# Linear attention with a gated FFN: attention's last product from eight quarter products to seven

## The chip, the cores and the metric

The kernel runs on one core of a Trainium2 chip. The metric is the device time of one execution in microseconds (us), as the median of several runs; a profiled execution of the same kernel gives the trace. Five engines work side by side, each through its own queue in order: TensorE (PE: matmuls and transposes; PEld is its weight load), VectorE (DVE), ScalarE (ACT), GpSimd (POOL) and SyncE (SP), from whose queue most transfers are issued.

## The reference, cut to what matters

The input `src` has 4 batch entries of 2048 tokens with 256 features, in float32. What is computed (16 heads of 64, `HD` = 1024; weights given, all biases and gains at work):

```
xn  = layernorm(src)
Q   = elu(xn Wq + bq) + 1 ;  K = elu(xn Wk + bk) + 1 ;  v = xn Wv + bv
KV  = per head and batch entry: sum over tokens of K^T v
Z   = 1 / (Q . sum over tokens of K + 1e-6)          per token and head
att = (Z Q KV) Wo + bo
x1  = layernorm(xn + att) * g1 + be1
s   = layernorm(x1 + gelu(x1 W1 + b1) W2 + b2) * g2 + be2
g   = silu( fp4_linear( silu(fp4_linear(xn, w_gate)) * fp4_linear(xn, w_up), w_down ) )
out = src + s * g
```

`fp4_linear` rounds its input and its weight to a grid of eight magnitudes, with one scale for each 16 values. KV needs all tokens of an entry before the first `att` of that entry can be computed.

## The kernel before, in words

**Tiling.** The tokens are worked on in 32 blocks `n` of 256 (two halves of 128, `TB` = 2), 8 for each of the entries `b = n // 8`. KV and Wo are multiplied together once per entry: M = blockdiag(KV) Wo is a 1024 x 256 matrix, and `att` of a block is (Z Q) M. M is kept in two tiles `m` of 128 x 4 x 256, one for each half `f` of the heads (`m_of_half`, L589-643; half 0 from four of the eight 128-row chunks of M, half 1 from the others).

**Stages.** A prologue computes the keys of entry 0 and quantizes the weights. Then the main loop (L1093-1222) runs over the 32 blocks. Beside block n of entry b < 3 it works on the keys of entry b+1, so that KV of the next entry is ready when its first block comes: two steps (`subs`) a block, first for the first half of the heads over the first four blocks, then for the second half over the last four, so n % 8 = 0 to 3 have other work beside them than n % 8 = 4 to 7. The last entry (n = 24 to 31) has no keys beside it.

TensorE executes everything in the order in which the program gives it (`mm`, L102, and `tr`, L105, keep the program order), so a block on TensorE is this sequence, with the names by which the profile knows the products:

- `pq` (L793): the block's queries from `xnT` and `wq_sb`, ahead of which stands `ffn_1` of the block before (`pf`, L877, first product of the FFN: `x1T` x `w1_sb`; ScalarE applies gelu to it and writes `hT`);
- `pk` (`keys_k`, L567) for the first step of keys, `pz` (`sums`, L815): the sums that Z is made of. VectorE adds epsilon and inverts, the result goes to DRAM (`z_d`) and comes back spread over partitions as `zb`;
- `pxk` (keys times values' inputs), `pg` (`gate_up` of block n+1, L732), `pd` (`down`, L757);
- then `qz` (L842) on VectorE: `zq <- zq * zb`, two operations of 128 x 1024. `zq` is Z Q, transposed;
- `pk` for the second step of keys, and on VectorE `kk` from it;
- `pa` (`attention`, L849): (Z Q) M, 16 products of 128 x 128 by 128 x 256 into one accumulator;
- `pxk` again, `py` (`ffn_2`, L924, second product of the FFN of block n-1), `pt_x` (`x1_T`, L865: x1 transposed), `pscale` (`spread_scales`: the scales of the fp4 grid, transposed, to DRAM and back), the rest of `py`, and `ffn_1`.

**VectorE and ScalarE** keep the program order in the prologue. In the main loop (`in_order` is False) a scheduler places their operations, and `issue_after` holds one behind a named other. Behind `pa` VectorE adds `xn` to it (`x1`), takes the statistics (`stats`; the power for 1/sqrt runs on GpSimd, `rstd` L430) and normalizes. `scales_h` and `scales_x` (L661) compute the scales of the fp4 grid for the next blocks: `scales_x(n + 2)` reads the tile `xn` of block n+2, which `load_xn` (L648) fetches on SP into the buffer that the sum for `x1` has just freed (two buffers). `keys_in` and `keys_apart` prepare the next step of keys: statistics and normalization on VectorE, or a fetch of what the first half already stored, then on ScalarE a column of ones and two copies (`apart`), and on SP a transposing transfer (`apartT`).

**The FFN's second product** is computed by seven products of quarters instead of eight: `w2_sums` (L218) forms four sums of quarters of W2 once on GpSimd, `ffn_sums` (L905) four sums of quarters of `hT` per block on VectorE (tile `hs`), `ffn_2` 28 products of 128 columns into seven quarters of two accumulators (`PY_SLOT`, L922), and `output` (L948) adds them with five additions (`s<-s,py`). The attention product is not computed in that way here.

**GpSimd** does the power for rstd, `gate_addend` (L778), `ffn_addend` (L785) and `attention_addend` (L652): additions and multiplications of 128 x 512. **Accumulators** (PSUM): a pool `mm` of four, a pool `acc` of two, a pool `pxk` of two.

Of the kernel before, what the change touches and what calls it, by code (L numbers as in the profile page):

```python
# [8 lines left out]
F32 = mybir.dt.float32  # L9
# [3 lines left out]
ALU = mybir.AluOpType  # L13
AX = mybir.AxisListType

P = 128
# [6 lines left out]
def linear_attention_gated_by_fp4_ffn(  # L23
# [38 lines left out]
    nc = tc.nc  # L62
    B, S, D = src.shape
# [5 lines left out]
    NH = HD // P  # L69
# [4 lines left out]
    TB = 2  # L74
# [14 lines left out]
    def mm_tile(name):  # L89
        return ps.tile([P, 512], F32, tag="mm", name=name)  # L90

    def acc_tile(name, tag="acc"):
        return pacc.tile([P, 512], F32, tag=tag, name=name)
# [8 lines left out]
    def mm(*args, **kw):  # L102
        return tc.keep_in_program_order(nc.tensor.matmul(*args, **kw))  # L103
# [105 lines left out]
    def w2(q):  # L209
        return w2_sb[:, W2_OF[q]]  # L210
# [375 lines left out]

    kh, m_sb = {}, {}

    def m_of_half(b, f, dep=None, ahead=False):  # L589


        nm = f"{b}_{f}"
        if wv_sb.get(f) is not None:
            wv = wv_sb.pop(f)
        else:
            wv = batch.tile([P, ND, HALF], F32, tag="wv", name=f"wv_{nm}", bufs=1)
            nc.sync.dma_start(wv, wv_d[f])
        wo = batch.tile([P, 4, D], F32, tag="wo", name=f"wo_{nm}", bufs=1)
        load_when(dep, wo, by_chunks(Wo)[:, 4 * f : 4 * f + 4, :])
        if ahead:  # L600
            yield
        if f == 0:
            kh[b] = batch.tile([P, NH, 32], F32, tag="kh", name=f"kh_{b}")
            nc.gpsimd.memset(kh[b], 0.0)
        m = m_sb[b, f] = batch.tile([P, 4, D], F32, tag="m", name=f"m_{nm}", bufs=3)
        pxk = keys.pop((b, "pxk", f))
        xk = batch.tile([P, ND, HALF], F32, tag="xk", name=f"xk_{nm}", bufs=1)
        for d in range(ND):
            scalar.copy(xk[:, d, :], pxk[d])

        k_d = dram.tile([1, HALF], F32, tag="k_d", name=f"k_d_{nm}", bufs=2)
        nc.sync.dma_start(k_d, xk[:1, 0, :])
        yield
        cols_ = k_d.rearrange("o (c i p) -> i p (o c)", c=4, i=2)
        for i in range(2):
            hs = slice(i * DH, (i + 1) * DH)
            nc.sync.dma_start(kh[b][hs, 4 * f : 4 * f + 4, 2 * f + i], cols_[i])
        yield

        pkv = mm_tile(f"pkv_{nm}")[:, : 4 * DH].rearrange("p (c f) -> p c f", c=4)  # L620
        kv = work.tile([P, 4, P], F32, tag="s", name=f"kv_{nm}", bufs=1)
        nc.gpsimd.memset(kv, 0.0)
        for ci in range(4):
            for d in range(ND):
                for h in range(2):
                    cs = slice(ci * P + h * DH, ci * P + (h + 1) * DH)
                    mm(
                        pkv[h * DH : (h + 1) * DH, ci, :], wv[:, d, cs], xk[:, d, cs],
                        start=d == 0, stop=d == ND - 1,
                    )  # L630
        for h in range(2):
            hs = slice(h * DH, (h + 1) * DH)
            scalar.copy(kv[hs, :, hs], pkv[hs])
        yield
        for c2 in range(2):
            pm = mm_tile(f"pm_{nm}_{c2}").rearrange("p (c d) -> p c d", c=2)
            for ci in range(2):
                mm(
                    pm[:, ci, :], kv[:, 2 * c2 + ci, :], wo[:, 2 * c2 + ci, :],
                    start=True, stop=True,  # L640
                )
            scalar.copy(m[:, 2 * c2 : 2 * c2 + 2, :], pm)
        yield


# [196 lines left out]
    def qz(n):  # L842
# [3 lines left out]
            ins = vector.tensor_tensor(zq[:, cs, :], zq[:, cs, :], zb[:, cs, :], ALU.mult)  # L846
        return ins.ins

    def attention(n):  # L849
        zq = blk[n].pop("zq")  # L850
        m = [m_sb[n // NB, f] for f in range(2)]
        pa = acc_tile(f"pa_{n}").rearrange("p (j d) -> p j d", j=TB)
        for j in range(TB):
            for c in range(NH):
                mm(
                    pa[:, j, :], zq[:, c, j * P : (j + 1) * P], m[c // 4][:, c % 4, :],
                    start=c == 0, stop=c == NH - 1,
                )
        x1 = work.tile([P, TB, D], F32, tag="x1", name=f"x1_{n}")
        vector.tensor_tensor(x1, blk[n].pop("xn"), pa, ALU.add)  # L860
        mv, rstd = stats(x1, f"1_{n}")
        normalize(x1, x1, mv, rstd)
        blk[n]["x1"] = x1
# [31 lines left out]
                )  # L895
        blk[n]["gelu"] = ins.ins

    def ffn_sums(n):  # L905
        hT = blk[n]["hT"]
        h = {
            f"{i + 1}{k + 1}": hT[:, k * NF2 : (k + 1) * NF2, i * P : (i + 1) * P]
            for i in range(2) for k in range(2)
        }  # L910
        t = work.tile([P, 4, NF2, P], F32, tag="zb", name=f"hs_{n}", bufs=1)
        s1, s2, s3, s4 = (t[:, i] for i in range(4))
        vector.tensor_tensor(s3, h["11"], h["21"], ALU.subtract)
        vector.tensor_tensor(s1, h["21"], h["22"], ALU.add)
        vector.tensor_tensor(s2, s1, h["11"], ALU.subtract)
        vector.tensor_tensor(s4, h["12"], s2, ALU.subtract)
        blk[n]["ffn"] = {
            1: (h["11"], "11"), 2: (h["12"], "21"), 3: (s4, "22"), 4: (h["22"], "t4"),
            5: (s1, "t1"), 6: (s2, "t2"), 7: (s3, "t3"),
        }  # L920

    PY_SLOT = {2: (0, 0), 3: (0, 1), 4: (0, 2), 1: (0, 3), 6: (1, 0), 7: (1, 1), 5: (1, 2)}  # L922

    def ffn_2(n, to, order=(1, 2, 4, 3, 5, 7, 6)):  # L924

        py = blk[n].setdefault("py", {})
        done = blk[n].get("done", 0)
        blk[n]["done"] = to
        for at in range(done, to):
            i, c = order[at // NF2], at % NF2  # L930
            bank, slot = PY_SLOT[i]
            if bank not in py:

                t = (mm_tile if (bank == 0) == (n >= NBLK - NB - 1) else acc_tile)(f"py{bank}_{n}")
                py[bank] = t.rearrange("p (s d) -> p s d", s=4)
            if "ffn" in blk[n]:
                h, w = blk[n]["ffn"][i]
            else:
                hT = blk[n]["hT"]
                h, w = {  # L940
                    1: (hT[:, :NF2, :P], "11"), 2: (hT[:, NF2:, :P], "21"),
                    4: (hT[:, NF2:, P:], "t4"),
                }[i]
            mm(
                py[bank][:, slot, :], h[:, c, :], w2(w)[:, c, :], start=c == 0, stop=c == NF2 - 1
            )

    def output(n):  # L948
        g, o, x1, py = (blk[n][k] for k in ("g", "o", "x1", "py"))
        s = work.tile([P, TB, D], F32, tag="s", name=f"s_{n}", bufs=1)  # L950

        def quarters(t):
            return t.rearrange("p j (h d) -> p (j h) d", h=2)

        def of(bank, slot, n):
            return py[bank][:, slot : slot + 1, :].to_broadcast([P, n, P])

        s4, x4 = quarters(s), quarters(x1)
        vector.tensor_tensor(s4, x4, py[0], ALU.add)
        vector.tensor_tensor(s4[:, :3, :], s4[:, :3, :], of(0, 3, 3), ALU.add)  # L960
        vector.tensor_tensor(s4[:, 1:, :], s4[:, 1:, :], of(1, 0, 3), ALU.add)
        vector.tensor_tensor(s4[:, 2:, :], s4[:, 2:, :], of(1, 1, 2), ALU.add)
        vector.tensor_tensor(s4[:, 1::2, :], s4[:, 1::2, :], of(1, 2, 2), ALU.add)
        mv, rstd = stats(s, f"2_{n}")
        for j in range(TB):
            vector.scalar_tensor_tensor(
                s[:, j, :], s[:, j, :], mv[:, j, 0:1], g[:, j, :], ALU.subtract, ALU.mult
            )
        for j in range(TB):
            vector.scalar_tensor_tensor(  # L970
                o[:, j, :], s[:, j, :], rstd[:, j : j + 1], o[:, j, :], ALU.mult, ALU.add
            )
        nc.sync.dma_start(rows_of(out, n), o)
# [119 lines left out]
    for n in range(NBLK):  # L1093
# [56 lines left out]
                down(n, j)  # L1150
        with tc.issue_after(blk[n + 1]["late"]) if n < last else nullcontext():
            qz_ins = qz(n)
        if not subs:
            ffn_2(n - 1, 4 if n < last else 8)
        kk_ins = keys_k(b + 1, subs[1]) if subs else qz_ins
        if n > 0:
            with tc.issue_after(kk_ins):
                ffn_sums(n - 1)
        attention(n)
        if n + 2 < NBLK:  # L1160
            load_xn(n + 2)
        if subs:
# [16 lines left out]
                scales_x(n + 2)  # L1179
        for sub in next_subs if n == 0 else ():  # L1180
            keys_in(bn + 1, sub)
        early = [sub for sub in next_subs[:1] if sub < NB]
        for sub in early:
            keys_apart(bn + 1, sub)
        x1_T(n)
        if not subs:
            ffn_addend(n, False)
        if n == last:
            gate_addend(n)
        for sub in next_subs[len(early) :]:  # L1190
            keys_apart(bn + 1, sub, blk[n]["act"])

        if n > 0 and not subs:
# [63 lines left out]
```

## Time and profile before

| what | value |
|---|---|
| median of 3 runs | 1907.02 us (1906.78 to 1907.91) |
| the profiled execution: its own time | 1906.97 us |
| its span in the trace | 1904.9 us |
| its granted TensorE clock | 0.997 of full speed |
| all chunks of `pa`, 1024 records | 227.0 us busy |
| VectorE busy / ScalarE busy / GpSimd busy | 1303.2 / 708.9 / 357.5 us |

The span is the time from the first to the last instruction on the core; the execution's own time has about 2 us around it. "Busy" adds up an engine's working time, and says nothing of whether its idle time cost anything. A float32 product appears in the trace as two records: 16 products of `pa` per block give 32 records, and 32 blocks 1024. In the groups of instructions, `pa<-m,zq 128*128 128x256 f32` reads: output `pa` from the inputs `m` and `zq`, a 128 x 128 weight against a moving operand of 128 partitions by 256 columns; behind it stand busy time and mean ns of one (the ends of pipelined matmuls are modelled, so for products the distance between starts is the better measure), and then the engine's idle time ahead of the group with what ended most of it. In a timeline line stand the start in us, the duration, the engine, the line and operation, how many of them are drawn together, and in brackets how long the engine had stood idle and for what.

### The profile page before, as it was taken

The page shows a single profiled execution, that of the slowest core. Times are in us where ns is not written, and L with a number is a line of the kernel's source. Part 1 is how long each engine was busy: PE and PEld are TensorE (multiplying, and loading weights), DVE is VectorE, ACT ScalarE, POOL GpSimd, SP SyncE. Part 2 cuts the span into 40 slices and gives each one's busy share as a digit, 9 for nine tenths or more (in the row PEclk, how much of TensorE's full clock was granted, in tenths as well). Part 3 has the DMA queues.
Part 4 walks back from the last instruction along what each step waited for, and adds up shares of the span by engine and source line. Part 5 has one row for each costly group of instructions (what it writes and reads, how often), then busy time and mean ns, then how long its engine had stood idle before and what let it go on. Part 6 is the DMA issues. An engine that isn't in the chain of part 4 may idle for free.

```text
span 1904.9 us, 23848 instructions
## 1 busy us (share of the span) xinstructions
PE 1875.4 (98%) x8772; PEld 1379.3 (72%) x8772; DVE 1303.2 (68%) x2338; ACT 708.9 (37%) x1191; POOL 357.5 (19%) x348
## 2 busy tenths in 40 slices
PE   9999999999999999999999999999999999999997
PEld 4456577767777777777777787677777688788876
DVE  5657667666666667666666666676666678888875
ACT  2334444334334344433243543353332333333332
POOL 1411222011121112220112210212110122222221
PEclk9999999999999999999999999999999999999999
DMA  5525555345434456544444553464442444445541
GB/s 182 190 78 112 116 105 108 97 106 96 93 64 89 110 102 126 132 80 95 88 87 78 115 103 102 91 137 89 95 83 69 78 80 88 82 84 93 91 81 42
DMA packets 228243, 187.62 MB, mean 98 GB/s; under 512 B 107656, under 2 KB 189844, under 8 KB 228127
## 3 DMA queue, kind: packets, MB, share of 16 engines
q1 hardware_dynamic: 227292, 184.53, 46.4%
q8 instruction: 69, 1.13, 0.3%
q10 hardware_dynamic: 834, 1.58, 0.3%
q14 instruction: 48, 0.39, 0.1%
HBM read 130.91 MB, written 32.59 MB: 86 GB/s over the span
## 4 chain that ended last, share of the span: by engine, by line
PE 90%; DVE 4%; DMA 2%; issue 1%; POOL 1%; ACT 0%; SPq 0%; POOLq 0%; ACTq 0%; DVEq 0%
PE pg L103 15%; PE pk L103 11%; PE pa L103 11%; PE pxk L103 11%; PE pf L103 11%; PE pq L103 11%; PE pd L103 8%; PE py L103 8%; PE pz L103 2%; DMA zb<-z_d 1%; DVE x L119 1%; DVE scale L119 1%; PE pt_x L106 1%; POOL rstd L430 1%; PE pm L103 1%
## 5 line engine op out<-in xcount | busy, mean ns | idle before, releaser
L430 POOL TENSOR_TENSOR rstd<-rstd,neg_half 128x2 f32<-128x2 f32 x96 | 72.6, 757 | 1450.2 <-DVE rstd L119 1015.0
L103 PE MATMUL pg<-wgu,qT 128*128 128x352 f32 x1024 | 311.0, 462 | 2.3 <-issue 2.2
L103 PEld LDWEIGHTS pg<-wgu,qT 128*128 128x128 f32 x1024 | 194.6, 191 | 120.2 <-issue 17.9
L103 PE MATMUL pk<-wk_sb,xnT_k 128*128 128x512 f32 x512 | 232.2, 596 | 1.5 <-ACT xnT_k L119 1.4
L103 PE MATMUL pf<-x1T,w_sb 128*128 128x256 f32 x1024 | 226.9, 380 | 3.6 <-DVE zq L119 2.7
L103 PE MATMUL pa<-m,zq 128*128 128x256 f32 x1024 | 227.0, 379 | 1.9 <-DVE zq L119 1.8
L103 PE MATMUL pq<-xnT,wq_sb 128*128 128x256 f32 x1024 | 226.5, 379 | 1.0 <-ACT hT L119 1.0
L103 PE MATMUL pxk<-kk,xn_k 128*128 128x512 f32 x496 | 227.4, 597 | 0.0
L103 PEld LDWEIGHTS pa<-m,zq 128*128 128x128 f32 x1024 | 193.5, 190 | 39.4 <-issue 11.2
L103 PEld LDWEIGHTS pq<-xnT,wq_sb 128*128 128x128 f32 x1024 | 194.3, 190 | 27.7 <-ACT hT L119 1.4
L103 PEld LDWEIGHTS pf<-x1T,w_sb 128*128 128x128 f32 x1024 | 191.8, 190 | 29.7 <-DVE zq L119 3.1
L119 DVE SCALAR_TENSOR_TENSOR kk<-ek,pk 128x512 f32<-128x512 f32 x128 | 85.9, 686 | 146.8 <-ACT ek L119 146.8
L103 PEld LDWEIGHTS pk<-wk_sb,xnT_k 128*128 128x128 f32 x512 | 97.5, 191 | 104.6 <-issue 97.8
L103 PE MATMUL pd<-wd,qT 128*128 128x256 f32 x768 | 172.8, 380 | 0.5 <-ACT wd L119 0.5
L119 ACT ACT_TABLE_LOAD x122 | 156.5, 1283 | 41.3 <-PE pk L103 26.3
L103 PEld LDWEIGHTS pd<-wd,qT 128*128 128x128 f32 x768 | 145.3, 190 | 25.7 <-DVE qT L119 1.6
L103 PEld LDWEIGHTS pxk<-kk,xn_k 128*128 128x128 f32 x496 | 91.3, 190 | 99.0 <-issue 92.1
L119 ACT ACTIVATE h<-pg 128x352 f32<-128x352 f32 x128 | 58.8, 460 | 213.3 <-PE pg L103 213.3
L119 DVE TENSOR_TENSOR h<-h,pg 128x352 f32<-128x352 f32 x128 | 66.1, 517 | 100.7 <-PE pg L103 99.2
L119 ACT ACTIVATE hT<-pf,bcol 128x256 f32<-128x256 f32 x256 | 105.7, 472 | 57.8 <-PE pf L103 57.1
L119 ACT ACTIVATE ek<-pk,neg_one 128x512 f32<-128x512 f32 x128 | 85.5, 686 | 110.0 <-PE pk L103 109.7
L103 PE MATMUL py<-w_sb,hs 128*128 128x128 f32 x1024 | 125.9, 275 | 0.0
(136 smaller groups left out, 2327.5 us busy)
## 6 DMA issues: line engine op xcount, KB each, us to landing
zb<-z_d SPq DMA_DIRECT2D x128, 256.0 KB, 6.0
qT<-scale_d SPq DMA_DIRECT2D x248, 128.0 KB, 5.4
x_k<-in_L_attn_src_dram SPq DMA_DIRECT2D x32, 256.0 KB
x<-in_L_attn_src_dram SPq DMA_DIRECT2D x32, 256.0 KB, 2.6
xn_d<-xn_k SPq DMA_DIRECT2D x32, 256.0 KB, 2.0
xn<-xn_d SPq DMA_DIRECT2D x32, 256.0 KB, 2.6
xnT_d<-xnT_k SPq DMA_DIRECT2D x32, 256.0 KB, 2.0
xnT<-xnT_d SPq DMA_DIRECT2D x32, 256.0 KB, 2.8
```

The lines of the kernel that those rows point to most:

```text
L103: return tc.keep_in_program_order(nc.tensor.matmul(*args, **kw))
L106: return tc.keep_in_program_order(nc.tensor.transpose(*args, **kw))
L119: ins = op(*args, **kw)
L430: pool["last"] = nc.gpsimd.tensor_tensor(rstd[:, j0:j1], rstd[:, j0:j1], neg_half[:, j0:j1], ALU.pow).ins
```

## The change

In entries 0, 1 and 2 (`in_seven`) attention's product takes the form that the FFN's second product already has; the last entry keeps the eight.

- `m_sums(b)`: when the second half of M is ready, GpSimd forms t1 to t4 from M's quarters, four operations of 128 x 512, once per entry. `m` becomes two tags: `m0` with two buffers for the first half of the heads, `m1` with one for the second, and a tile `mt` for three of the sums; t1 is written over a quarter of M.
- `attention_sums(n)`: right behind `qz`, VectorE forms four sums of quarters of `zq` (128 x 512 each), three into a new tile `zs` and one over a quarter of `zq`.
- `attention(n)`: 28 products of 128 columns in place of 16 of 256, into two accumulators (one from `acc`, one from `mm`), and five additions in place of one for `x1`.
- Order: in block 0 attention goes ahead of the second step of keys. `keys_apart` of the next block's first step was called ahead of `x1_T`; now all of them follow it, behind `x1T` on ScalarE.
- The FFN's product is written with the same helpers as before in other words (`halves`, `seven_sums`, `seven_products`, `add_seven`); of its sums the order of the first two changes.

```diff
+    def in_seven(b):
+        return b < B - 1
+
+    def m_sums(b):
+        m = {
+            f"{k + 1}{j + 1}": m_sb[b, k][:, :, j * P : (j + 1) * P]
+            for k in range(2) for j in range(2)
+        }
+        t = batch.tile([P, 3, 4, P], F32, tag="mt", name=f"mt_{b}", bufs=1)
+        t1, (t2, t3, t4) = m["12"], (t[:, i] for i in range(3))
+        nc.gpsimd.tensor_tensor(t3, m["22"], m["12"], ALU.subtract)
+        nc.gpsimd.tensor_tensor(t1, m["12"], m["11"], ALU.subtract)
+        nc.gpsimd.tensor_tensor(t2, m["22"], t1, ALU.subtract)
+        nc.gpsimd.tensor_tensor(t4, m["21"], t2, ALU.subtract)
+        m_sb[b] = {"11": m["11"], "21": m["21"], "22": m["22"], "t1": t1, "t2": t2, "t3": t3, "t4": t4}
...
-        m = m_sb[b, f] = batch.tile([P, 4, D], F32, tag="m", name=f"m_{nm}", bufs=3)
+        m = m_sb[b, f] = batch.tile([P, 4, D], F32, tag=f"m{f}", name=f"m_{nm}", bufs=2 - f)
...
+        if f > 0 and in_seven(b):
+            m_sums(b)
         yield
...
+    SLOT = {2: (0, 0), 3: (0, 1), 4: (0, 2), 1: (0, 3), 6: (1, 0), 7: (1, 1), 5: (1, 2)}
+    WEIGHT = {1: "11", 2: "21", 3: "22", 4: "t4", 5: "t1", 6: "t2", 7: "t3"}
+    FOUR = NH // 2
...
+    def seven_sums(h, s1, s2, s3, s4):
+        vector.tensor_tensor(s1, h["21"], h["22"], ALU.add)
+        vector.tensor_tensor(s3, h["11"], h["21"], ALU.subtract)
+        vector.tensor_tensor(s2, s1, h["11"], ALU.subtract)
+        ins = vector.tensor_tensor(s4, h["12"], s2, ALU.subtract)
+        return {1: h["11"], 2: h["12"], 3: s4, 4: h["22"], 5: s1, 6: s2, 7: s3}, ins.ins
+
+    def seven_products(banks, left, weights, order, lo, hi):
+        for at in range(lo, hi):
+            i, c = order[at // FOUR], at % FOUR
+            bank, slot = SLOT[i]
+            mm(
+                banks[bank][:, slot * P : (slot + 1) * P], left[i][:, c, :],
+                weights(WEIGHT[i])[:, c, :], start=c == 0, stop=c == FOUR - 1,
+            )
+
+    def add_seven(dst, x, banks):
...
+        s4, x4 = quarters(dst), quarters(x)
+        vector.tensor_tensor(s4, x4, banks[0].rearrange("p (s d) -> p s d", s=4), ALU.add)
+        vector.tensor_tensor(s4[:, :3, :], s4[:, :3, :], of(0, 3, 3), ALU.add)
+        vector.tensor_tensor(s4[:, 1:, :], s4[:, 1:, :], of(1, 0, 3), ALU.add)
+        vector.tensor_tensor(s4[:, 2:, :], s4[:, 2:, :], of(1, 1, 2), ALU.add)
+        vector.tensor_tensor(s4[:, 1::2, :], s4[:, 1::2, :], of(1, 2, 2), ALU.add)
+
+    def attention_sums(n):
+        h = halves(blk[n].pop("zq"))
+        t = work.tile([P, 3, FOUR, P], F32, tag="zs", name=f"zs_{n}", bufs=1)
+        blk[n]["zs"], ins = seven_sums(h, t[:, 0], t[:, 1], h["21"], t[:, 2])
+        return ins
...
     def attention(n):
...
         x1 = work.tile([P, TB, D], F32, tag="x1", name=f"x1_{n}")
-        vector.tensor_tensor(x1, blk[n].pop("xn"), pa, ALU.add)
+        xn = blk[n].pop("xn")
+        b = n // NB
+        if in_seven(b):
+            pa = [acc_tile(f"pa0_{n}"), mm_tile(f"pa1_{n}")]
+            seven_products(
+                pa, blk[n].pop("zs"), lambda q: m_sb[b][q], (1, 2, 4, 3, 5, 7, 6), 0, 7 * FOUR
+            )
+            add_seven(x1, xn, pa)
...
             qz_ins = qz(n)
+        if in_seven(b):
+            attention_sums(n)
         if not subs:
             ffn_2(n - 1, 4 if n < last else 8)
+        if n == 0:
+            attention(n)
         kk_ins = keys_k(b + 1, subs[1]) if subs else qz_ins
         if n > 0:
             with tc.issue_after(kk_ins):
                 ffn_sums(n - 1)
-        attention(n)
+            attention(n)
...
-        early = [sub for sub in next_subs[:1] if sub < NB]
-        for sub in early:
-            keys_apart(bn + 1, sub)
         x1_T(n)
...
-        for sub in next_subs[len(early) :]:
+        for sub in next_subs:
             keys_apart(bn + 1, sub, blk[n]["act"])
```

## Prediction before the run

> **What bounds the kernel now.** I read the page's busy shares first, then busy time by stage (one block per stretch), then the groups by form, and last the timeline of single blocks, because only there one sees which wait ends last.
>
> ```profile
> PE 1875.4 (98%) x8772; PEld 1379.3 (72%) x8772; DVE 1303.2 (68%) x2338; ACT 708.9 (37%) x1191; POOL 357.5 (19%) x348
> ```
> ```profile
> core 0: us, PE busy (x) PEld busy (x) DVE busy (x) ACT busy (x) POOL busy (x), PEclk, DMA share, GB/s
> 474.44:531.54 57.10, 57.10 (x263) 42.10 (x262) 37.36 (x64) 19.59 (x34) 9.27 (x8) 1.00 0.45 89
> 649.71:706.81 57.10, 57.10 (x263) 42.10 (x262) 40.05 (x78) 24.08 (x40) 10.65 (x10) 1.00 0.53 105
> ```
> TensorE is busy for all of a middle block (57.10 of 57.10 us, clock 1.00): each us taken from its queue is a us gained, and each wait put into it is a us lost. VectorE has 17 to 20 us free per block, but that is a sum; what counts is where it stands when TensorE needs it.
>
> ```profile
> L103 PE MATMUL pa<-m,zq 128*128 128x256 f32 x1024 | 227.0, 379 | 1.9 <-DVE zq L119 1.8
> L119 DVE SCALAR_TENSOR_TENSOR o<-s,rstd,o 128x256 f32<-128x256 f32 x64 | 88.5, 1420 | 18.8 <-POOL rstd L430 18.8
> L119 DVE TENSOR_TENSOR s<-s,py 128x384 f32<-128x384 f32 x64 | 35.3, 551 | 29.2 <-PE py L103 28.2
> ```
> The first row is the product to be replaced, 32 records a block. The second (1420 ns, where the like-sized s<-s,mv,g takes 486) shows VectorE while GpSimd works on 128x512 operands: about 0.93 us more for each operation. The third is what an addition from PSUM costs.
>
> Block 4 of the timeline (entry 0, the first block beside which the second half of the next keys is worked on):
>
> ```profile
> 409.33 1.22 DVE L119 TENSOR_TENSOR zq<-zq,zb 128x1024 f32<-128x1024 f32 x1 [3.47 <-DMA zb<-z_d]
> 415.68 0.89 DVE L119 SCALAR_TENSOR_TENSOR h<-h,rs_h 128x704 f32<-128x704 f32 x1
> 417.18 7.07 PE L103 MATMUL pa<-m,zq 128*128 128x256 f32 x32
> 417.73 1.28 DVE L119 SCALAR_TENSOR_TENSOR kk<-ek,pk 128x512 f32<-128x512 f32 x2 [1.15 <-ACT ek L119]
> 424.09 3.60 PE L103 MATMUL pxk<-kk,xn_k 128*128 128x512 f32 x8
> 424.29 0.69 DVE L119 TENSOR_TENSOR x<-xn,pa 128x512 f32<-128x512 f32 x1 [2.62 <-PE pa L103]
> 425.00 0.32 SPq L650 DMA_DIRECT2D xn<-xn_d  x1
> 427.00 0.74 DVE L119 TENSOR_SCALAR x<-x,mv,rstd 128x256 f32<-128x256 f32 x2 [0.82 <-POOL rstd L430]
> 427.52 2.84 PE L103 MATMUL py<-w_sb,hT 128*128 128x128 f32 x24
> 427.65 0.68 DVE L119 TENSOR_REDUCE scale<-xn 128x32 f32<-128x512 f32 x1
> 431.99 0.60 PE L106 MATMUL pt_x<-ident,x 128*128 128x128 f32 x4
> ```
> Here x1 is normalized at 427.74 and transposed (pt_x) at 431.99: 4.2 us of slack. Ahead of attention VectorE waited 3.47 us for zb, so it is late: its last operation ahead of kk ends at 416.57, 0.61 us before attention starts. The reduction scale<-xn reads a transfer issued 2.65 us earlier and does not wait.
>
> **The change, part by part.** I count from attention's first matmul (0) in each block.
>
> *TensorE.* 16 matmuls of 256 columns become 28 of 128, two records each. Row: pa runs from 417.18 to 424.09, 6.91 us, 216 ns a record. The same form as the new ones is py: 40 records from 427.52 to 431.99, 4.47 us, 111.5 ns. So 56 x 0.1115 = 6.24: 0.66 us less a block. Against this stands the Trainium skill, "TensorE: Matmul & The Clock Gate", section "Back-to-back issue gap": the spacing of matmuls is set by weight load and product together, about 81 ns at 128 columns and 131 at 512, so short ones pay dearly. Interpolated, 256 columns cost 98, and 28 x 81 over 16 x 98 is 1.45: attention would take 10.0 us, and 24 blocks 74 us more (an estimate from that page). The row has this kernel's own type and shapes and halves with the columns; I take the row. 23 blocks give -15.1; block 0 is told apart below.
>
> *VectorE ahead of attention.* Four sums of 128x512, from the rows of hs (four take 2.76 us with their gaps). They stand behind the second zq<-zq,zb, ahead of h<-h,rs_h and kk. Attention's fourth product (record 24, at 2.68) needs the last sum. In blocks with early zb (n = 1, 2, 3, 7, 9, 10, 11 and so on) VectorE idled 3.1 to 3.6 us before kk, which hides the sums. In the late ones, n = 4, 5, 6 in each entry, it idled 0.2 to 1.3 us; the last sum comes at 2.0 to 2.5, still just in time, but kk and ffn_sums behind it move back.
>
> *VectorE behind attention.* One addition of 688 ns becomes five (starts 0, 0.72, 1.31, 1.90, 2.36; end 2.80). Built, the queue has a further difference: scale<-xn stands before the fifth, and in n = 3 to 6 of each entry also the reciprocal and y<-xn,rs_x stand before x1's rstd. scale<-xn waits for xn of block n+2, whose buffer is free only after the first addition: a wait in the middle of x1's chain. The reduction started 2.65 to 2.74 us after the issue in these blocks; I take 2.70.
>
> Chain of a late block, A being the first addition: its end A+0.69, issue, landing, reduction at A+3.41; reduction, fifth addition, scale to bn_stats +1.37; bn_stats to end of normalization 2.73 measured, +1.01 for reciprocal and y: A+8.52. A follows the four hs sums: end of h<-h,rs_h before (call it E) + 2.79 + 1.20 + 2.77, so 6.75+E. E was -0.61, 0.05, -0.67 (n = 4, 5, 6), 0.36, -0.20, -0.16 (12 to 14), -0.23, -0.75, -0.40 (20 to 22). TensorE now reaches pt_x at 6.24+3.43+4.46 = 14.13 and needs the second half of x1 at 14.24. The waits, A+8.57-14.24, are 0.3 to 1.4 us, sum **+7.1 us**. Behind pt_x are queued pscale, the rest of py and ffn_1, so all of it is lost; x1T on ScalarE waits with them.
>
> *Other blocks.* With early zb, A is 4.5 and normalization ends near 12.4 (n = 3: 13.0), before 14.13: hidden by pxk and py. In n = 1, 2, 7 to 10, 15 to 18 the keys' statistics follow, and xn_k, its store and ScalarE's copy move 1.2 us back. Dropping the early keys_apart puts x1T ahead of apart: that ends the one 0.88 us wait of pf for x1T (block 7), **-0.9**. But two copies then stand ahead of the table load before hT. I get the first hT pair at 23.1, and pq, which now takes pf's buffer (pa1 uses one more of the four), wants it at 23.37. Margin 0.3: I book **+0.7** for eight blocks. Bounds: 0 to 8 (1 us each). Of the moved SP issues, scale_d and the first qT go ahead of apartT; the latter's readers are over 8 us away, cost 0 to 1, taken 0.
>
> *GpSimd: M's sums.* Four 128x512 operations after M's second half, three times. Rows of the same size alone: 1.27 to 1.45 us, with w2_sums 1.45 to 1.93. They must be done at 1.8 (third product, t4); in block 8 M lands at -7.8, and 4 operations with VectorE in between take about 8 us, ending near 0.6. But VectorE's zq and three sums are held 1 us each: E goes from -3.5 to 3.3, the last sum to 2.5. A is 7.2, normalization ends at 15.1: 0.9 at pt_x, and the hT chain, 2.7 later, costs pq 1.5. Blocks 8 and 16: **+4.8** (bounds 0, if VectorE is not held, and 9).
>
> *Block 0.* attention now goes ahead of keys_k and x1's chain has no ffn_2 over it: pxk waits for kk behind the additions. I put ffn_1 about 4 to 5 us later than its 197.2. In the trace pg of the next block starts at 223.2 after waiting 2.2 us for transfers and then takes 11.4 us instead of 9.5, so most is absorbed: **+1.0** (-1 to +4).
>
> Sum: -15.1 - 0.9 + 7.1 + 0.7 + 4.8 + 1.0 = **-2.4 us**. The profiled execution took 1906.97 us (span 1904.9 and 2.1 around it), 0.05 below the median, so the same sum holds for the runs: **1904.6**. A measurement of this kernel tells about 0.2% (3.8 us) from no change.
>
> **Rivals.**
> - *Hidden after all (28%).* If x1 is ready at 14.2 also in the late blocks and GpSimd hardly holds VectorE, what is left is -15.1 - 0.9 + 1 + 1: 1893. For it: TensorE binds everywhere and VectorE has 17 us free. Against: the queue order, which puts a transfer's landing into x1's chain.
> - *The landing decides (24%, slower).* In the last entry the same reduction had to wait:
>
> ```profile
> 1660.80 0.34 SPq L650 DMA_DIRECT2D xn<-xn_d  x1
> 1664.64 0.69 DVE L119 TENSOR_REDUCE scale<-xn 128x32 f32<-128x512 f32 x1 [0.51 <-DMA xn<-xn_d]
> ```
> That is 3.84 us after the issue. With it each late block loses 1.14 more (+10.3), and eight blocks about 0.9 at pq (+7): 1922. Slower than 0.2% begins at about 3.2 us from issue to reduction. Against it: 2.65 to 2.74 in all twelve blocks n = 3 to 6.
> - *Short matmuls do not halve (3%).* By the page's spacing 1981; py's rows speak against it.
>
> The forecast has 45%, spread over 1900 to 1909: 0.17 of it faster by over 0.2%, 0.26 within, 0.02 slower. With rival one faster, the second and third slower but for 0.02: faster 0.45, within 0.28, slower 0.27. The range, 1890 to 1915, takes in all of the hidden case and the forecast with its bounds, and leaves out the worse part of the second rival and the third.
>
> **What would show it.** pa's 56 records in 6.2 us a block. In n = 4, 5, 6 a wait of PE pt_x for DVE x of 0.3 to 1.4 us, and scale<-xn waiting for DMA xn; none in n = 9 to 11. In blocks 8 and 16 VectorE operations of 1.7 to 2.2 us under GpSimd's sums, and pt_x and pq waiting. If pt_x never waits, the first rival holds; if pq waits for hT in n = 1, 2, 7 to 10, my margin of 0.3 us was wrong.

## The result, and the profile after

The changed kernel takes **1897.45 us** (median of 4 runs, 1896.17 to 1898.94) against 1907.26 before: ratio 0.9949, 95% interval 0.9931 to 0.9966. Run again later on, beside other kernels, it took 1894.16 (1892.76 to 1897.45) against 1906.55: ratio 0.9938, 0.9924 to 0.9951. So it is 10 to 12 us faster, where the prediction had -2.4 as the likeliest and -14 for its first rival. The range held the time and the sign was right, but the size came out nearer to the rival: the range had been drawn to take in the rival's case as well, so that it held says nothing for the sum.

The busy shares, then busy time by stage (the columns as before; first the block that began at 474.44 us before, then the one at 649.71):

```profile
PE 1864.5 (98%) x9348; PEld 1385.3 (73%) x9348; DVE 1396.8 (74%) x2530; ACT 706.7 (37%) x1191; POOL 384.0 (20%) x360
```
```profile
473.04:529.73 56.69, 56.69 (x286) 42.33 (x285) 41.70 (x75) 19.58 (x34) 9.27 (x8) 1.00 0.44 87
646.15:702.60 56.45, 56.45 (x287) 42.27 (x286) 44.37 (x87) 23.80 (x40) 11.14 (x10) 1.00 0.52 107
```
TensorE still fills the block; the second block is 0.65 us shorter, as `pa`'s rows said. VectorE works 4.3 us more in each and still has 12 to 15 us free.

The groups by form, for the new products, the additions, and two operations that wait for a transfer (idle time before the group at the end of the line):

```profile
L103 PE MATMUL pa<-mt,zq 128*128 128x128 f32 x384 | 50.7, 275 | 0.0
L119 DVE TENSOR_TENSOR x<-x,pa 128x384 f32<-128x384 f32 x48 | 26.6, 554 | 15.1 <-PE pa L103 13.6
L119 DVE TENSOR_REDUCE scale<-xn 128x32 f32<-128x512 f32 x32 | 21.8, 682 | 16.2 <-DMA xn<-xn_d 16.0
L119 ACT COPY xn_k<-ones 128x2 f32<-128x2 f32 x55 | 9.3, 195 | 18.1 <-DMA xn_d<-xn_k 18.0
```
The reduction waits for `xn` of block n+2, as foreseen (0.5 us in all before). The last row is one that the prediction did not cost: ScalarE's `ones` (the column of ones) overwrites a part of `xn_k` and so waits for the store of `xn_k` to DRAM. Before, this row had even more idle time:

```profile
L119 ACT COPY xn_k<-ones 128x2 f32<-128x2 f32 x55 | 9.3, 195 | 122.7 <-DMA xn_d<-xn_k 122.6
```
But that was the first key step's `ones`, ahead of `x1T`, where nothing was kept waiting by it except in block 7 (the 0.88 us wait that the prediction names); the second step's waited 0.3 us at the most in blocks 1 to 22. Now it is the second step's that waits, with other work queued behind it.

Block 4 of the timeline again, the VectorE chain and `pt_x`:

```profile
416.55 0.88 DVE L119 SCALAR_TENSOR_TENSOR h<-h,rs_h 128x704 f32<-128x704 f32 x1
416.60 1.95 PE L103 MATMUL pa<-m,zq 128*128 128x128 f32 x16
421.07 0.68 DVE L119 TENSOR_TENSOR x<-xn,pa 128x512 f32<-128x512 f32 x1
424.43 0.69 DVE L119 TENSOR_REDUCE scale<-xn 128x32 f32<-128x512 f32 x1 [0.38 <-DMA xn<-xn_d]
425.04 0.41 DVE L119 TENSOR_TENSOR x<-x,pa 128x256 f32<-128x256 f32 x1
428.18 0.74 DVE L119 TENSOR_SCALAR x<-x,mv,rstd 128x256 f32<-128x256 f32 x2 [0.82 <-POOL rstd L430]
430.75 0.60 PE L106 MATMUL pt_x<-ident,x 128*128 128x128 f32 x4
```
The reduction stands between the fourth and fifth addition and waits for its transfer; but x1 is normalized at 428.92 and `pt_x` starts at 430.75 without waiting, 1.8 us later.

Where TensorE does wait, five of the rows (who for whom, us in total, times, longest; waits of up to 0.15 us are not in them):

```profile
PE pq L103 <- ACT hT L119: 3.3, 2, 1.8
PE pf L103 <- DVE s L119: 1.8, 3, 1.2
PE pd L103 <- DVE qT L119: 1.3, 2, 0.8
PE pf L103 <- ACT x1T L119: 0.5, 1, 0.5
PE pt_x L106 <- DVE x L119: 0.5, 1, 0.5
```
`pt_x` waits once, in the last block. New are `pf` for `s` (n = 2, 10, 15), `pq` for `hT` in n = 16 (1.55 us; in n = 0 it was 0.95 before and is 1.75) and `pd` for `qT` (n = 23 and 25).

To see where time goes, I cut every trace at the first `pa` of certain blocks (us; single profiled executions):

| kernel | to block 1 | 1 to 23 | 23 to 24 | 24 to 31 | rest |
|---|---|---|---|---|---|
| before | 243.1 | 1271.4 | 50.7 | 304.8 | 35.0 |
| changed | 243.0 | 1261.3 | 51.8 | 306.1 | 35.0 |
| changed, again (e5) | 242.0 | 1258.2 | 51.8 | 305.7 | 35.1 |
| e1 products only | 241.6 | 1255.8 | 50.1 | 305.6 | 35.0 |
| e2 longer x1 | 244.0 | 1262.5 | 51.7 | 305.4 | 35.1 |
| e3 no M sums | 240.0 | 1259.4 | 51.7 | 305.6 | 34.9 |
| e4 py swapped | 243.2 | 1256.2 | 50.1 | 304.0 | 35.1 |
| e6 ones later | 243.2 | 1256.0 | 51.7 | 305.5 | 35.0 |
| e7 early apart | 242.1 | 1257.7 | 50.1 | 304.0 | 34.8 |
| e8 scale behind | 240.1 | 1255.8 | 51.8 | 304.7 | 35.4 |
| e9 block 0 | 243.6 | 1259.2 | 51.7 | 305.4 | 35.0 |
| e10 scale, swap | 240.0 | 1255.8 | 50.0 | 306.0 | 35.0 |
| e11 all entries | 240.4 | 1255.8 | 51.8 | 330.0 | 38.8 |
| e12 all three | 242.1 | 1255.8 | 50.1 | 305.4 | 35.0 |

The first column scatters by 4 us, without order, so sums of whole runs hide what the second column shows to 0.1 us. There the full gain is 15.6 us (1255.8); the change got 10.1 in one execution and 13.2 in another. At full gain (e8) each block from 1 to 22 is 0.66 us shorter than before, and block 7 by 1.8. The stretch from 24 to 31, whose products are unchanged, scatters too, by 2 us without e11. So the first profile's -7.7 us is about -10.1 in blocks 1 to 23, +1.0 in 23 and +1.3 behind it.

### The profile page after: what moved, and what is told of

Read it like the earlier page. It is cut to its first block, busy times and chain, and to the rows that moved or that the text cites. A ratio compares the mean times of both kernels' runs of the same rounds, so it can differ in the third digit from the quotient of the medians.

```text
span 1897.2 us, 25223 instructions
## 1 busy us (share of the span) xinstructions
PE 1864.5 (98%) x9348; PEld 1385.3 (73%) x9348; DVE 1396.8 (74%) x2530; ACT 706.7 (37%) x1191; POOL 384.0 (20%) x360
## 4 chain that ended last, share of the span: by engine, by line
PE 81%; DVE 9%; DMA 6%; issue 2%; POOL 1%; ACT 1%; SPq 0%; ACTq 0%; POOLq 0%; DVEq 0%
PE pg L103 14%; PE pq L103 10%; PE pk L103 10%; PE pxk L103 10%; PE pa L103 9%; PE pf L103 9%; PE pd L103 8%; PE py L103 7%; PE pz L103 2%; POOL rstd L430 1%; DMA xn_d<-xn_k 1%; DVE x L119 1%; DMA zb<-z_d 1%; DMA xn<-xn_d 1%; DVE scale L119 1%
## 5 line engine op out<-in xcount | busy, mean ns | idle before, releaser
L430 POOL TENSOR_TENSOR rstd<-rstd,neg_half 128x2 f32<-128x2 f32 x96 | 76.8, 801 | 1352.2 <-DVE rstd L119 1039.2
L119 ACT ACTIVATE x1T<-pt_x,bcol 128x256 f32<-128x256 f32 x64 | 32.7, 561 | 357.4 <-PE pt_x L106 357.4
L119 DVE SCALAR_TENSOR_TENSOR zq<-e,pq 128x512 f32<-128x512 f32 x128 | 84.2, 683 | 61.9 <-ACT e L119 61.8
L119 ACT ACTIVATE hT<-pf,bcol 128x256 f32<-128x256 f32 x256 | 103.8, 476 | 50.1 <-PE pf L103 49.6
```

The source lines that it names most:

```text
L119: ins = op(*args, **kw)
L430: pool["last"] = nc.gpsimd.tensor_tensor(rstd[:, j0:j1], rstd[:, j0:j1], neg_half[:, j0:j1], ALU.pow).ins
```

## The experiments

My theory after the first trace: the transfer in x1's chain is there, but no late block is late; the missing 3 to 5 us are lost in the blocks with the first half of the keys, at `pf` and `pq`. Rivals: the loss is in the added work itself (sums, additions, GpSimd); or in the buffers; or it is chance.

**e1, products only.** The sums of zq and of M and four of the five additions are left out (the edit of M's sums is that of e3):

```diff
-        if in_seven(b):
-            attention_sums(n)
...
+            h = halves(blk[n].pop("zq"))
+            left = {1: h["11"], 2: h["12"], 3: h["12"], 4: h["22"], 5: h["21"], 6: h["21"], 7: h["11"]}
...
-            add_seven(x1, xn, pa)
+            vector.tensor_tensor(x1, xn, pa[0].rearrange("p (j d) -> p j d", j=TB), ALU.add)
```


> This kernel keeps the 28 products of 128 columns and leaves out everything else that the seven need: the four sums of zq (quarters of zq stand in for them), the four sums of M on GpSimd (quarters of M stand in), and four of the five additions (only the first accumulator is added); so att is not the reference's. Theory A (what is missing from the full gain is lost to the sums and additions): 24 blocks at 0.66 us less and the 0.8 us wait of pf for x1T in block 7 gone make -16.6; with about 1 us left for block 0's order, 1891 to 1892 us against 1907.3 before and 1897.5 for the whole change. Theory B (the short products themselves cost TensorE something outside of pa's rows, and sums and additions are free): no better than the whole change, 1897 us.

Measured: 1890.08 us (1889.19 to 1891.25), ratio 0.9914 (0.9901 to 0.9928). Theory A. The short products bring what the row promised: 24 x 0.66 + 0.8 = 16.6 expected, 15.8 measured, of it 15.6 in blocks 1 to 23.

**e2, a longer x1.**

```diff
     add_seven(x1, xn, pa)
+    for _ in range(2 if 4 <= n % NB <= 6 else 0):
+        vector.tensor_tensor(x1, x1, x1, ALU.max)
```


> The changed kernel with two more operations of 128x512 on VectorE (x1 = max(x1, x1), twice 0.69 us, result unchanged) between the fifth addition and the statistics of x1, in n = 4, 5, 6 of entries 0 to 2 alone. Theory A (the chain with the transfer in it is as the prediction described, but ends 0.2 to 2 us before TensorE comes to pt_x, by the trace at 12.3, 14.4, 14.5, 13.9, 13.6, 14.0, 13.0, 13.6, 12.8 us after the first product where about 14.2 is needed): the part of 1.4 us that goes beyond the slack is lost, 0, 1.4, 1.4, 1.0, 0.7, 1.1, 0.1, 0.8, 0 us, together +6.5: 1904 us. Theory B (x1 is far from deciding): 0, 1897.5. Theory C (pt_x already waits in each of these blocks, as forecast): nine times 1.4, 1910 us.

Measured: 1899.10 us, ratio 0.9958 (0.9942 to 0.9973); in the trace the nine blocks lose 3.8 us, and `pt_x` waits:

```profile
PE pt_x L106 <- DVE x L119: 1.8, 4, 0.6
```
Between A and B: next to nothing was waiting before (0.6 us in the nine blocks), and little slack was left. It is little more than half of A's 6.5: two 0.69 us operations moved the end of x1's chain, counted from the first addition, by 1.0 us only (9.1 against 8.1 on average), since the transfer landed 0.3 us earlier and the built order puts the reciprocal and y, which had lengthened the way from the statistics to the normalization (3.4 us on average, 2.7 now), between and behind them.

**e3, no M sums.**

```diff
-        nc.gpsimd.tensor_tensor(t3, m["22"], m["12"], ALU.subtract)
...
-        m_sb[b] = {"11": m["11"], "21": m["21"], "22": m["22"], "t1": t1, "t2": t2, "t3": t3, "t4": t4}
+        m_sb[b] = {"11": m["11"], "21": m["21"], "22": m["22"], "t1": m["12"], "t2": m["22"], "t3": m["12"], "t4": m["21"]}
```


> The changed kernel without the four sums of M's quarters on GpSimd (quarters of M stand in for t1 to t4, so att is not the reference's); the order on the other engines is unchanged. Theory A (they hold VectorE's operations, and that costs only where the chain to hT is short, in block 16 with 1.8 us): 1895.6 us, pq no longer waits for hT in block 16. Theory B (the forecast's +4.8 in blocks 8 and 16 is in the measured time): 1892.7. Theory C (the wait in block 16 has another cause, the transfer of xn_k to DRAM): no change, 1897.5.

Measured: 1893.14 us, ratio 0.9929 (0.9916 to 0.9941), which overlaps the interval of the changed kernel in both its runs. As a number this is theory B's, but against the first profile 3.0 us of the difference lie ahead of block 1, in the stretch that scatters. In block 16, with no sums on GpSimd at all, the wait is still there:

```profile
1120.12 0.19 ACT L119 COPY xn_k<-ones 128x2 f32<-128x2 f32 x1 [3.11 <-DMA xn_d<-xn_k]
1124.77 1.56 PE L103 MATMUL pq<-xnT,wq_sb 128*128 128x256 f32 x6 [1.30 <-ACT hT L119]
```
So it is theory C by the trace: the wait does not need the M sums. They add to it at times: in block 16 of the first profile x1's first addition came at 5.3 us after attention, without them at 4.3, but in e5, with them, at 4.4.

**e4, py's accumulators swapped.**

```diff
-    kinds = (mm_tile, acc_tile) if n >= NBLK - NB - 1 else (acc_tile, mm_tile)
+    kinds = (mm_tile, acc_tile)
```


> The changed kernel with py's two accumulators swapped between the pools in n < 23: the first, which is read out after two additions, from the pool mm that pf takes its accumulators from, the second from the other. Order on every engine unchanged. Theory A (since pa's second accumulator comes from mm, the last pf takes the one of py that is free only after the fifth addition of s, and waits 0.3 to 1.2 us in n = 2, 10 and 15 by the trace): these waits go, -2.5 us at most, 1895 us. Theory B (ScalarE's hT is as late in these blocks, so pq waits instead of pf): no change, 1897.5 us.

Measured: 1890.44 us, ratio 0.9915 (0.9902 to 0.9929). Theory A in kind: no `pf` waits for `s` any more, and blocks 1 to 23 take 1256.2 us. In n = 2 `hT` starts at 22.6 us after attention as before, and `pq` waits by 0.1 only. It gained more than 2.5, since block 16 happened to land early here (below) and the stretches from block 23 on came out 3.8 us shorter.

**e5, the changed kernel again.**

> The changed kernel once more, to see which of its losses come back. By the trace of the first profile the main loop between the attention of block 1 and that of block 23 lost 5.2 us of its full gain (n = 2, 5, 6, 7, 9, 10, 15, 16), and block 23 1.7 us. Theory A (the waits of pf for s and the long landings of xn_k's store in n = 2 and n = 16 belong to this kernel's order): n = 2 and n = 16 lose over 1 us each again, the time is 1897 us (ratio 0.995). Theory B (they are the luck of one execution): they are elsewhere or gone, and a time as low as 1891 to 1893 can come.

Measured: 1894.16 us. n = 2 lost 1.2 us again (theory A), n = 16 nothing this time (theory B): `ones` came at 18.5 us after attention, not at 20.5. The wait is in the order, its length varies from execution to execution.

**e6, ones later.** `keys_apart` of the second key step goes behind all `hT`:

```diff
-        for sub in next_subs:
+        for sub in next_subs[:1]:
             keys_apart(bn + 1, sub, blk[n]["act"])
...
+        for sub in next_subs[1:]:
+            keys_apart(bn + 1, sub, blk[n]["gelu"])
```


> The changed kernel with keys_apart of the second key step of each block (ones, and in the blocks with the first half of the keys the copies apart) behind all hT on ScalarE, instead of behind x1T. ScalarE's ones there waits for xn_k's store to DRAM, and m_h and hT are queued behind it. Theory A (this wait delays hT, which starts at 21.5 to 24.2 us after attention in n = 1, 2, 7 to 10, 15 to 18 against 20.9 before, and with it pq in n = 16, and the fifth addition of s behind m_h that pf waits for in n = 2, 10, 15): hT starts at 21.0 or earlier there, no pf or pq waits in these blocks, -3 to -4.5 us against the change, 1893 to 1894.5. Theory B (pf's and pq's waits come from the buffers alone): pf still waits for s in n = 2, and the time stays at 1897.

Measured: 1891.95 us (1890.62 to 1893.28), ratio 0.9923, 2.2 below e5 on the same chip. `hT` starts at 19.6 to 20.8 us after attention, `pf` waits nowhere for `s`, and `pq` only by 0.2 us in n = 16. Blocks 1 to 23: 1256.0, the full gain. Theory A.

**e7, early apart.** The call ahead of `x1_T` restored:

```diff
+        early = [sub for sub in next_subs[:1] if sub < NB]
+        for sub in early:
+            keys_apart(bn + 1, sub)
         x1_T(n)
```


> The changed kernel with keys_apart of the first key step put back ahead of x1_T, as before the change. Theory A (the prediction's step: behind the five additions xn_k is stored about 0.8 us later, so the ones on ScalarE wait and x1T's second half behind them): pf waits for x1T by about 0.8 us in n = 7 as before and by 0.3 to 1 us in n = 2, 9 and 16, together +2 to +3.5 us, 1900 us. Theory B (ScalarE has room enough): within 1 us of the change, 1897.

Measured: 1892.65 us (1890.52 to 1893.63), ratio 0.9927 (0.9914 to 0.9939), not slower; blocks 1 to 23 take 1257.7 us, 0.5 less than in e5. Theory B. The scheduler now put only `ones` between the two halves of x1T, and the copies behind both, so this undoes the call, not the old order; that x1T must not stand behind copies is not contradicted.

**e8, scale behind.** The landing taken out of x1's chain:

```diff
-                scales_x(n + 2)
+                with tc.issue_after(blk[n]["norm"]):
+                    scales_x(n + 2)
```


> The changed kernel with scale<-xn (and what follows from it) held behind the normalization of x1, so that the landing of xn of block n+2 is no longer inside x1's chain. Theory A (by the trace x1 was ready before TensorE came to pt_x in all late blocks but n = 5 and 6): x1's normalization ends 1 to 2 us earlier after attention, but only 0.6 us are gained, 1896.8. Theory B (the late blocks lose the +7.1 of the prediction, hidden in another wait): -7, 1890. Theory C (pscale, which needs scale, becomes late instead): pscale waits for scale, up to 0.5 us in each late block, +3.

Measured: 1889.67 us (1888.74 to 1890.49), ratio 0.9912 (0.9899 to 0.9926), 4.5 below e5 (2.4 of it between blocks 1 and 23, 1.9 in the stretch before, which scatters). That is B's number in another place. No late block but n = 5 and 6 had been waiting at `pt_x`; but in blocks n = 1, 2, 7 to 10, 15 to 18 x1 is normalized at 11.1 us after attention in place of 11.7 to 12.9, and with it the keys' xn_k is stored earlier, `ones` no longer waits, and `hT` is on time. Block 16 before this edit (changed kernel: the store's issue, then ScalarE, then TensorE):

```profile
1121.51 0.32 SPq L474 DMA_DIRECT2D xn_d<-xn_k  x1
1125.05 0.19 ACT L119 COPY xn_k<-ones 128x2 f32<-128x2 f32 x1 [2.45 <-DMA xn_d<-xn_k]
1125.15 0.78 ACT L119 ACTIVATE m_h<-h 128x704 bf16<-128x704 f32 x1
1127.51 1.28 ACT L119 ACT_TABLE_LOAD   x1
1128.80 2.66 ACT L119 ACTIVATE hT<-pf,bcol 128x256 f32<-128x256 f32 x7
1129.69 1.56 PE L103 MATMUL pq<-xnT,wq_sb 128*128 128x256 f32 x6 [1.55 <-ACT hT L119]
```
and with it:

```profile
1113.06 0.32 SPq L475 DMA_DIRECT2D xn_d<-xn_k  x1
1115.13 0.20 ACT L119 COPY xn_k<-ones 128x2 f32<-128x2 f32 x1
1115.23 0.78 ACT L119 ACTIVATE m_h<-h 128x704 bf16<-128x704 f32 x1
1118.89 2.30 ACT L119 ACTIVATE hT<-pf,bcol 128x256 f32<-128x256 f32 x6
```
The store leaves at 16.9 us after attention in the first and at 15.0 in the second, `hT` follows at 24.2 and at 20.9. In the first, `m_h` and the table load stand behind a landing.

**e9, block 0 in its old order.**

```diff
-        if n == 0:
-            attention(n)
         kk_ins = keys_k(b + 1, subs[1]) if subs else qz_ins
...
-            attention(n)
+        attention(n)
```


> The changed kernel with block 0 in the order before the change: the second step of keys first, then attention. The stretch from block 0's attention to block 1's took 58.22 us before and 58.54 and 60.01 in two profiles of the changed kernel, with pxk waiting 1.8 and 3.3 us for kk behind x1's additions. Theory A (the new order costs what the prediction booked, +1.0, or more): this stretch takes 57.6 (58.22 less 0.66), pxk does not wait, -1 to -2.4 us against the second run of the changed kernel (1894.2): 1892 to 1893. Theory B (the first stretch is set by transfers, and attention ahead of the keys costs nothing): within 0.5 us of it.

Measured: 1894.31 us (1890.06 to 1896.81), ratio 0.9929 (0.9915 to 0.9943). Theory B. My 57.6 us compared two different stretches, for in the old order `pk`'s 3.4 us lie ahead of attention. Up to block 1 the old order takes 243.6 us, the new one 243.0 and 242.0: `pt_x` waits 1.7 us for x1 where `pxk` had waited for `kk`.

**e10, scale behind and py swapped; e12, and block 0.**

> The changed kernel with scale<-xn behind x1's normalization and py's accumulators swapped, together. Theory A (both remove the same loss, one at its source and one where TensorE met it, and with either the main loop from block 1 to 23 already runs at its full gain): no better than either alone, 1889 to 1890.5 us. Theory B (they remove different waits): their gains of 4 to 6 us add up, 1884 to 1886.

> The changed kernel with all three: scale<-xn behind x1's normalization, py's accumulators swapped, block 0 in the order before. Theory A: the main loop at its full gain and block 0 at 57.6 us, 1888 to 1889 us, the best of all. Theory B (block 0's order is free): the same as without it, 1889 to 1890.5.

Measured: e10 1889.43 us (1888.70 to 1890.76), ratio 0.9913 (0.9899 to 0.9926); e12 1890.33 us (1889.23 to 1891.97), ratio 0.9917 (0.9904 to 0.9931). Theory A for e10: the gains do not add, they are one loss met at two places, and blocks 1 to 23 stay at 1255.8 us. Theory B for e12. e8 and e10 cannot be told apart, and have the lowest times found, about 17 us below the kernel before.

**e11, all four entries.**

```diff
     def in_seven(b):
-        return b < B - 1
+        return True
```


> The changed kernel with scale<-xn behind x1's normalization and with the seven products in the last entry too (M's sums for it on GpSimd as well). Theory A (there no keys cover the time between attention and pt_x: in the trace x1 is ready at 10.5 us and pt_x starts at 10.5, and the second half of zq comes only 1.5 us after attention begins, so the sums of zq stop attention by about 1.6 us and the additions make x1 about 1.8 us later): each of seven blocks loses 2 to 3 us and gains 0.66, +10 to +17, 1900 to 1907 us. Theory B (TensorE binds there too): -5.3, 1884.5.

Measured, with e8's edit in it: 1924.32 us, ratio 1.0090 (1.0075 to 1.0105), 35 us above e8. Theory A's mechanism, at twice its size:

```profile
PE pa L103 <- DVE zs L119: 17.4, 8, 2.4
PE pt_x L106 <- DVE x L119: 5.1, 8, 2.2
PE pa L103 <- DVE zq L119: 4.6, 8, 1.3
```
These three are 27.1 us; once, in n = 24, attention also waits 1.6 us for M's sums on GpSimd. `zs` costs 2.2 us a block rather than 1.6, because the scheduler laid sums of hT between those of zq, and attention also waits for zq itself, since `zq<-zq,zb` for the second half of the heads, which ends 1.6 us after attention begins (n = 27), is in time for the fifth of 16 products (1.7 us in) but late for the second of the seven (0.9).

## Why the prediction was right or wrong, point by point

- **TensorE, -15.1 and -0.9: right.** e1 and e8 measure 15.6 for blocks 1 to 22: 22 times 0.66, and 1.2 more in block 7. The page's spacing (the Trainium skill, "TensorE: Matmul & The Clock Gate", "Back-to-back issue gap") would have made the products dearer; here 56 records take 6.25 us against 6.91 for 32.
- **VectorE behind attention, the late blocks, +7.1: wrong in size; this is the step that failed.** The mechanism was there in each of the nine blocks: the reduction waits for its transfer in the middle of x1's chain. But x1 was normalized 12.3 to 14.5 us after attention began, on average 13.6, where the sum had 15.0; two blocks lost 0.6 us together in one execution, none in the next. The missing 1.4 us came in two terms. I added the four sums of zq at 2.79 us; they cost VectorE 2.0 (in block 4, second `zq<-zq,zb` to the end of `h<-h,rs_h`: 2.40 us before, 4.40 after; 2.1 on average). The lines show why; first before, then after:

```profile
414.08 0.88 DVE L119 TENSOR_REDUCE scale<-h 128x44 f32<-128x704 f32 x1
414.99 0.19 DVE L119 TENSOR_SCALAR scale<-scale 128x44 f32<-128x44 f32 x1
415.22 0.43 DVE L119 RECIPROCAL rs_h<-scale 128x44 f32<-128x44 f32 x1
```
```profile
412.94 0.88 DVE L119 TENSOR_REDUCE scale<-h 128x44 f32<-128x704 f32 x1
413.74 0.68 DVE L119 TENSOR_TENSOR zs<-zq 128x512 f32<-128x512 f32 x1
414.34 0.18 DVE L119 TENSOR_SCALAR scale<-scale 128x44 f32<-128x44 f32 x1
414.45 0.69 DVE L119 TENSOR_TENSOR zq<-zq 128x512 f32<-128x512 f32 x1
415.06 0.68 DVE L119 TENSOR_TENSOR zs<-zs,zq 128x512 f32<-128x512 f32 x1
415.67 0.42 DVE L119 RECIPROCAL rs_h<-scale 128x44 f32<-128x44 f32 x1
416.00 0.62 DVE L119 TENSOR_TENSOR zs<-zq,zs 128x512 f32<-128x512 f32 x1
```
Before, each operation needs the one ahead of it and starts 0.03 to 0.04 us after its end. After, the sums stand between, and each operation starts 0.07 to 0.09 us before the end of the one ahead: 0.1 us saved at each of seven steps. From `h<-h,rs_h` to the first addition it took 3.6 us where I had 4.0, so this came at 5.5 us on average, not 6.5. And from there the chain took 8.1 us, not 8.5: from the reduction to the statistics 1.05 us in place of 1.37. By the prediction's own signs the first rival held in these blocks. (The waits were summed with A+8.57 where the chain had given A+8.52, 0.4 us of the 7.1.)

- **The landing, 2.70 us: right on average, not as a constant, and in part by luck.** From its issue the reduction came 2.6 to 2.9 us later in seven of the nine blocks, and 3.8 and 3.3 in n = 6 and 21: 2.9 on average, and 2.6 in e5. The second rival's 3.84 occurred once. What I had read off before, 2.65 to 2.74, was no landing: the reduction did not wait there, so it was only an upper bound.
- **GpSimd, +4.8: too much.** In block 8 nothing was lost. VectorE was held, `zq<-zq,zb` for 2.29 us in n = 16 and a sum for 1.75 (0.68 alone), in line with the exclusive port pair that the Trainium skill describes ("SBUF — State Buffer", "SBUF: two separate sides"). But it ended earlier: h<-h,rs_h at 0.6 and 1.7 us, where I had 3.3. The 1.5 us that I booked at pq did appear in block 16 once, but e3 has 1.3 there without any sums, and e8 and e10, with them, lose nothing in either block.
- **pq waiting for hT, +0.7, and the moved wait: right place, wrong cause.** I expected the two apart copies ahead of the table load to decide. What delays hT is `ones`, which overwrites a column of xn_k and so waits for its store; I had moved xn_k, its store and ScalarE's copy 1.2 us back without asking what waits for the store. Behind it stand m_h, and on VectorE in the order after m_h the fifth addition of s, which pf waits for, because attention's second accumulator has changed the rotation of the buffers. This cost 4.9 us in the first profile (n = 2, 7, 9, 10, 15, 16) and 2.4 in e5's.
- **Dropping the early keys_apart, -0.9:** the wait of pf in n = 7 is gone, but e7 keeps it away with the call restored. What the two share is the place of the copies behind x1T.
- **Block 0, +1.0: not to be seen** in a stretch that scatters by 4 us (e9).
- **Not foreseen:** block 23 to 24 takes 1.0 us more than before, though it should take 0.66 less, in eight of the thirteen profiles of changed kernels, both of the unaltered change among them; the last section follows it up.

## What to carry to other kernels

Operations that are put between dependent small ones on the same engine can cost less than their sum: read in the timeline how soon an operation follows one that it needs and one that it doesn't (here 0.04 us after its end and 0.08 before), and subtract the difference for each step. When a step moves back, follow its stores too: whoever overwrites the stored tile waits for the landing, and what is queued behind that write waits with it. A transfer that gives work its input should not be waited for inside another chain; here taking one reduction out of it was worth 2.4 us against one execution and 5.5 against another.

## What the hardware showed that I had not expected

A store of 256 KB was over, for the operation that overwrites its source, 2.1 to 2.9 us after its issue in eight of the ten blocks of the changed kernel where ScalarE waits for it, but 3.5 us in n = 2 and n = 16, and 4.4 in n = 16 of e3. An estimate by the Trainium skill ("SBUF — State Buffer", "The DMA setup-cost knee": some 2 us fixed, and the bytes by 436 GB/s) is 2.6: right to 0.6 us for most, and 1 to 2 us short where it mattered. In n = 2 the wait was 3.2 to 3.5 us in all seven profiles in which the store leaves late and `ones` waits for it (the changed kernel twice, e2, e3, e4, e7, e9). In n = 16 it was 2.1 to 4.4 us in the same seven, and in the four with over 3 us a packet of 16 KB on another queue, q8, which the profile's list of queues calls `instruction`, began and ended between the issue and the landing; in the other three none did. In n = 2 there is none, and why the wait is long there stays open.

In block 23 the landing of the scales takes 1.6 to 1.7 us in five profiles of variants and before, and 2.7 to 3.6 in eight; first the changed kernel, then e4, the store's issue and that of the reads which wait for it:

```profile
1520.31 0.34 SPq L725 DMA_DIRECT2D scale_d<-scaleT  x1
1523.89 1.28 SPq L728 DMA_DIRECT2D qT<-scale_d  x3
```
```profile
1515.36 0.34 SPq L725 DMA_DIRECT2D scale_d<-scaleT  x1
1516.95 3.18 SPq L728 DMA_DIRECT2D qT<-scale_d  x7
```
3.58 us against 1.59, with the same issue time within the block (16.0 us after attention). Between these two issues lies, again, a packet of q8 in the first case, and none in the second (queue: packets, MB, share of the DMA engines):

```profile
q1 hardware_dynamic: 144, 0.07, 6.7%
q8 instruction: 1, 0.02, 2.7%
```
```profile
q1 hardware_dynamic: 144, 0.07, 13.7%
```
In all eight long cases this packet ends 17.5 to 18.3 us after attention, and the reads start 1.1 to 1.2 us behind its end. In the five short ones among the variants it is over at 16.5, before the store's first packet at 16.8. So the long landing goes with this packet; what sets its time stays open. Where the landing is long, `pd` waits 0.8 us for `qT` and the stretch takes 51.7 us in place of 50.1, whatever the length between 2.7 and 3.6. The traces show why it is always the same: VectorE's first `qT<-qT,gridT` starts at 28.4 to 28.5 us after attention in the short cases, under GpSimd's `x<-x,g_r`, and ends at 29.5, 0.8 us after that operation's end. In the long ones it starts at 29.6 to 30.2, under the next, `x<-x,shift_r`, and ends at 31.2, again 0.8 us after that one's end: 1.7 us later, as the stretch is.
